# Row layout of an expert pair and the widths of its down product

## The chip, the cores and the metric

The kernel runs on one core of a Trainium2 chip. The metric is the device time of one launch in microseconds; lower is better. Every launch computes the whole model, so there is no warm part that is left out.

## The reference, cut to what matters

The model has eight residual blocks on x of 4 x 256 tokens with 256 features. The change touches only the last, a mixture of 64 experts in which each token goes to eight:

```python
def _L3_ffn_ref(hidden_states, gate_w, gate_proj_w, up_proj_w, down_proj_w):
    B, S, H, I, E, K = (2, 128, 256, 96, 64, 8)
    x = hidden_states.reshape(-1, h)                 # 1024 tokens
    router_logits = x @ gate_w
    routing_weights, selected = jax.lax.top_k(router_logits, K)
    routing_weights = jax.nn.softmax(routing_weights, axis=-1)
    ...
    gate = jax.lax.ragged_dot(hidden_sorted, gate_proj_w, group_sizes)
    up = jax.lax.ragged_dot(hidden_sorted, up_proj_w, group_sizes)
    down = jax.lax.ragged_dot(jax.nn.silu(gate) * up, down_proj_w, group_sizes)
    ...
    out = jnp.sum(out * routing_weights[..., None], axis=1)
    return out.reshape(b, s, h)
...
x = x + _L3_ffn_ref(_layernorm(x, axis=-1), ...)
```

So there are 8192 pairs of token and expert, 128 for an expert on average. Gate and up go from 256 features to 96, down goes from 96 back to 256.

## The kernel before

Everything up to the experts (the other seven blocks, and the routing of the eighth) is recorded by `Flow`, a small planner: each operation names its engine, an estimated cost, what it reads and what it writes, and the planner fixes one order for each engine. The routing stands in `tile3`, which runs once for each of the eight tiles of 128 tokens. It ends with the row numbers. `sel` marks the chosen experts, a product with a triangle of ones (L1599) gives `pos`, the place of a token among those of its expert, and `first` holds a number for each expert, made once at the start by an iota (L323). VectorE computes `ok` (L1604: chosen, and place under CAP = 192), then `v = first - pos` (L1606), times `ok` (L1607); `max` sorts the eight values of a token (L1608). The row of a choice is `slots = NROWS - v` (L1615). After that come `m` (L1622) and ACT's exponential (L1627) for the weights of the choices, and POOL's indirect DMAs (L1677), eight a tile, which scatter the normed tokens to the rows of `hs` in HBM. A last column of each row, HW = 257, holds the index of the result in `yd`; rows that no token takes hold an index out of bounds, so that nothing is written for them.

Each expert has 192 rows of `hs`, two experts are a pair, and there are 32 pairs. A count of choices that found no row (L1791 to L1797) decides whether a general path is run; it is not run here. From L1766 on PSUM and SBUF are laid out anew, and the order on PE, ACT, DVE, POOL and SP is as written. For each pair p:

- `load_rows` (L1779) brings the pair's 384 rows as [128 partitions, RPP = 3 rows]: partition q has the rows 3q, 3q+1 and 3q+2. Rows are consecutive by expert, so partitions 0 to 63 hold the first expert and 64 to 127 the second.
- `rows_turned` (L1839) turns them with six TensorE transposes to `hbT` [feature, j, q], copied out of PSUM by ACT (L1923) and DVE (L1924), one pair ahead.
- gate and up (L1912): for each of the two experts two matmuls each with 96 weight columns and 192 moving columns, which are hbT's three runs of 64. f32 throughout.
- ACT's silu gives `g` (L1918), DVE's product `act` (L1920), of shape [96, 2, 3, 64].
- the down product (L1930): for each j of 3 and each expert i, act[:, i, j, :] (96 x 64) is the stationary operand and the expert's down weights (96 x 256) move; the result goes to rows i*64 to i*64+63 of the PSUM tile `y`. j = 0 and 1 share one tile, j = 2 has another.
- the copies out of PSUM to `yb` (L1935; ACT has j = 1), and three indirect DMAs of POOL (L1937), which put the 128 rows of each j to `yd` by the indices in the loaded rows. Those indices lie in the same partitions and the same j as the results.
- SP then issues the load of the rows of pair p + 6, the weights of later experts, and at certain pairs loads of finished results from `yd`, which DVE (L1873) and PE (L1878) add to x with their weights.

On PE, the order inside the loop is: gate and up of pair p, the transposes of pair p + 1, the down product of pair p.

Of the kernel before, what the change touches and what calls it, by code (L numbers as in the profile page):

```python
# [23 lines left out]
I32 = mybir.dt.int32  # L24
AF = mybir.ActivationFunctionType
ALU = mybir.AluOpType
AX = mybir.AxisListType

P = 128
# [17 lines left out]
E3, I3, K3 = 64, 96, 8  # L47
ORDERED = {mybir.EngineType.PE, mybir.EngineType.DVE, mybir.EngineType.Activation,
           mybir.EngineType.Pool}
GROUP, WEIGHTS, FIRST = 4, 6, 2  # L50
# [5 lines left out]
ON_PE = (3, 4, 5, 6, 7)  # L56
CAP = 192
RPP = 2 * CAP // P
NROWS = E3 * CAP
NPAIR = NTOK * K3  # L60
NSTAGE = 9
# [169 lines left out]
def model(ctx: ExitStack, tc: tile.TileContext, a: dict, out: bass.AP):  # L231
    nc = tc.nc
    PSUM = bass.MemoryType.PSUM

    const = ctx.enter_context(tc.tile_pool(name="const", bufs=1))
# [11 lines left out]
    def held(pool, shape, name, dtype=F32):  # L247
        return pool.tile(shape, dtype, tag=name, name=name)
# [4 lines left out]
    def x_t(t):  # L253
# [20 lines left out]

    hs = dram.tile([NROWS, HW], F32, tag="hs", name="hs")
    yd = dram.tile([NPAIR, D], F32, tag="yd", name="yd")
# [10 lines left out]
    q1 = [q1_both[:, k, :] for k in range(2)]  # L287
    q12 = held(early, [P, 2 * RPP * HW], "q12", BF16)
    q2 = [held(early, [P, 2 * I2], f"q2{k}", BF16) for k in range(3)]
# [28 lines left out]
        channel_multiplier=-1,  # L318
    )
    onesb = held(const, [P, P], "onesb", BF16)  # L320
    nc.gpsimd.memset(onesb, 1.0)
    first_i = held(const, [P, E3], "first_i", I32)
    nc.gpsimd.iota(first_i, pattern=[[-CAP, E3]], base=NROWS, channel_multiplier=0)  # L323
    first = held(const, [P, E3], "first")
    nc.vector.tensor_copy(first, first_i)
    sel = held(const, [P, NT, E3], "sel", BF16)
    rwo = held(const, [P, NT, E3], "rwo")
# [3 lines left out]
    for j in range(K3):  # L331
        nc.gpsimd.memset(bound[:, j : j + 1], float(NROWS - BOUND[j] * CAP))
    choice_w = held(const, [P, NT, K3], "choice_w")
# [24 lines left out]
    ps = banks.tile([P, 2, NT], F32, tag="bank0", name="ps_far")  # L358
# [56 lines left out]
    def layers(nk):  # L415
# [25 lines left out]
        def bank(shape, name):  # L441
            return ("bank", shape, name)
# [31 lines left out]
        def loader():  # L474
# [18 lines left out]
            def simple(name, c):  # L493
# [1061 lines left out]
        def tile3(t, q, lane, left):  # L1555
# [9 lines left out]
            y = yield Op(PE, 3.5, (u, BO3), new=[bank([P, D], "ps_y")])  # L1565
# [9 lines left out]
            rows = hx.ap.rearrange("p (j d) -> p j d", j=K3)  # L1575
# [5 lines left out]
            hT, rest = w[:, :D].rearrange("p (c r) -> p c r", c=2), w[:, D + E3 : D + 2 * E3]  # L1581
            lg, ok, v = w[:, D : D + E3], w[:, D + 2 * E3 : D + 3 * E3], w[:, D + 3 * E3 : D + 4 * E3]
# [14 lines left out]
            ps = yield Op(PE, 0.06 * (t + 1), SEL[: t + 1], new=[bank([P, E3], "ps_pos")])  # L1597
# [4 lines left out]
            pos, places = ps.ap, Buf()  # L1602
            yield Op(DVE, 1.4, (ps, SEL[t]), (places,))
            nc.vector.scalar_tensor_tensor(ok, pos, float(CAP), sel[:, t, :], ALU.is_lt, ALU.mult)  # L1604

            nc.vector.tensor_sub(v, first, pos)  # L1606
            nc.vector.tensor_mul(v, v, ok)  # L1607
            nc.vector.max(top[:, 8 : 8 + K3], v)  # L1608

# [3 lines left out]
            nc.vector.tensor_reduce(spilt, rest[:, 1 : 1 + K3], AX.X, ALU.max)  # L1613
            nc.vector.tensor_scalar(rest[:, 0:1], spilt, float(NROWS), float(NROWS), ALU.mult, ALU.add)
            nc.vector.tensor_scalar(  # L1615
# [55 lines left out]
        def scatter(t, hx, rows, row_data, places, at):  # L1671
            for j in range(K3):
# [6 lines left out]
                    out_offset=bass.IndirectOffsetOnAxis(ap=slots[:, t, j : j + 1], axis=0),  # L1679
                    in_=rows[:, j, :], in_offset=None, bounds_check=NROWS - 1, oob_is_err=False,  # L1680
                )
# [43 lines left out]
    def ps_mm(shape, name):  # L1725
        return psum.tile(shape, F32, tag="mm", name=name, bufs=4)
# [4 lines left out]
    def ps_acc(shape, name):  # L1731
        return psum.tile(shape, F32, tag="acc", name=name, bufs=2)
# [19 lines left out]
    def moe_tile(shape, tag, bufs):  # L1752
        return moe.tile(shape, F32, tag=tag, name=tag, bufs=bufs)
# [4 lines left out]
    def load_weights(k):  # L1758
# [31 lines left out]
    ps = ps_acc([P, NT], "ps_over")  # L1790
# [6 lines left out]
    with tc.If(rv > 0):  # L1797
# [7 lines left out]
        with tc.For_i(0, E3, 1) as e:  # L1805
            dn = moe_tile([I3, D], "dn_left", 1)
            nc.sync.dma_start(dn, a["w3_dn"][:, bass.ds(e, 1), :].rearrange("p e d -> p (e d)"))
            gu = moe_tile([P, 4 * I3], "gu_left", 1)
            nc.sync.dma_start(gu, a["w3_gu"][:, bass.ds(e, 1), :, :].rearrange("p e k i -> p (e k i)"))
            for c in range(NCH):  # L1810
                pg, pu = ps_mm([I3, CH], "ps_g3"), ps_mm([I3, CH], "ps_u3")
# [6 lines left out]
                g = moe_tile([I3, CH], "g_left", 1)  # L1818
                nc.scalar.activation(g, pg, AF.Silu)
                nc.vector.tensor_mul(g, pu, g)  # L1820
                for k in range(TPC):
                    t = c * TPC + k
                    y = ps_acc([P, D], "ps_y")
# [10 lines left out]
    def rows_turned(p):  # L1834
        hb, hbT = hbs[p], moe_tile([P, 2, RPP, P], "hbT", 2)
        tps = [ps_tp([P, RPP, P], "tp_hb") for _ in range(2)]
        for dc, tp in enumerate(tps):
            for j in range(RPP):
                nc.tensor.transpose(tp[:, j, :], hb[:, j, dc * P : (dc + 1) * P], ident)  # L1839
        return hbT, tps  # L1840
# [54 lines left out]
    def experts():  # L1895
        for p in range(in_early, AHEAD):
            load_rows(p)
        load_weights(FIRST)
        load_weights(FIRST + 1)

        nc.scalar.activation(silu, mhalf, AF.Silu)
        hbT, tps = rows_turned(0)
        nc.scalar.copy(hbT[:, 0], tps[0])
        nc.vector.tensor_copy(hbT[:, 1], tps[1])
        for p in range(n_pairs):
            e = 2 * p
            gu, dn = weights[e // GROUP]
            pg, pu = ps_mm([I3, 2, RPP, P // 2], "ps_g3"), ps_mm([I3, 2, RPP, P // 2], "ps_u3")
            for k, ps in enumerate((pg, pu)):
                for i in range(2):  # L1910
                    for dc in range(2):
                        nc.tensor.matmul(  # L1912
                            ps[:, i], gu[:, (e + i) % GROUP, 2 * k + dc, :],
                            hbT[:, dc, :, i * (P // 2) : (i + 1) * (P // 2)],
                            start=dc == 0, stop=dc == 1,
                        )
            g = moe_tile([I3, 2, RPP, P // 2], "g4", 2)
            nc.scalar.activation(g, pg, AF.Silu)  # L1918
            act = moe_tile([I3, 2, RPP, P // 2], "act3", 2)
            nc.vector.tensor_mul(act, pu, g)  # L1920
            if p + 1 < n_pairs:
                hbT, tps = rows_turned(p + 1)
                nc.scalar.copy(hbT[:, 0], tps[0])  # L1923
                nc.vector.tensor_copy(hbT[:, 1], tps[1])  # L1924
            yb = moe_tile([P, RPP, D], "yb", 3)
            for js in ((0, 1), (2,)):
                y = ps_acc([P, len(js), D], "ps_y")
                for k, j in enumerate(js):
                    for i in range(2):
                        nc.tensor.matmul(  # L1930
                            y[i * (P // 2) : (i + 1) * (P // 2), k], act[:, i, j, :],
                            dn[:, (e + i) % GROUP, :], start=True, stop=True,
                        )
                for k, j in enumerate(js):
                    (nc.scalar.copy if j == 1 else nc.vector.tensor_copy)(yb[:, j, :], y[:, k, :])  # L1935
            for j in range(RPP):
                put = nc.gpsimd.indirect_dma_start(  # L1937
                    out=yd[:, :],
                    out_offset=bass.IndirectOffsetOnAxis(
                        ap=hbs[p][:, j, D : D + 1].bitcast(I32), axis=0  # L1940
                    ),
                    in_=yb[:, j, :], in_offset=None, bounds_check=NPAIR - 1, oob_is_err=False,
                )
                tc.declare_no_dep(put.ins, group="back", reason="distinct rows")
                tc.add_to_no_dep_group("back", put.ins)
                backs.append(put.ins)

            n = len(on_pe)
            for t, j in on_pe[p * n // n_pairs : (p + 1) * n // n_pairs]:
                nc.vector.tensor_scalar(  # L1950
                    diag[:, t // 2, j - ON_PE[0], :], ident, choice_w[:, t, j : j + 1], None, ALU.mult
                )
            if p + AHEAD < n_pairs:
                load_rows(p + AHEAD)
            k = FIRST + 2 + p if p < WEIGHTS - 2 else p // 2 + WEIGHTS if p % 2 else 0
            if k and k < E3 // GROUP:
                load_weights(k)
# [113 lines left out]
```

## Time and profile before

| what | value |
|---|---|
| median of 4 runs | 686.26 us |
| lowest and highest | 678.46 and 688.81 us |
| the profiled execution | 680.24 us |
| its span, first to last profiled instruction | 678.5 us |
| granted TensorE clock, mean | 0.965 |
| PE busy, weight loads busy | 609.1 us (90%), 469.5 us (69%) |
| DVE, ACT, POOL busy | 462.4, 349.5, 401.3 us |
| down product L1930 | 384 PE instructions, 395 ns each (388 with the first pairs' weights) |
| gate and up L1912 | 512 PE instructions, 326 to 339 ns each, those of the first pairs to 419 |

The time is 1.7 us above the span in the profiled execution. A matmul's recorded duration runs until its result is out; the distance from one start to the next is shorter, since matmuls overlap. A weight load (PEld) is listed beside the matmul that uses it. In a timeline the first column is the start in us, the second the length from first start to last end of a group, "x12" the number of instructions in it, and the bracket the idle time before it with what ended it. The experts' stage lies from 488 us, where the first transposes start, to 659 us, where the last put is issued; the sum of the results follows until 675 us.

### The profile page before, as it was taken

What the parts mean: (1) busy time and instruction counts of PE and PEld (TensorE: products, weight loads), DVE (VectorE), ACT (ScalarE), POOL (GpSimd) and SP (SyncE); (2) the same over time, 40 slices, a digit from 0 to 9 for tenths busy, and PEclk for the clock granted to TensorE, in tenths of its full rate; (3) what the DMA queues carried; (4) which work ended last, traced back from release to release, by engine and by line L of the source; (5) the groups of instructions that cost most, each with busy time, mean ns of one, the idle gap of its engine ahead of it and who ended that gap; (6) DMA issues with size and microseconds to landing.
All of it is one profiled execution on the core that took longest, in us unless ns stands there. A gap on an engine that the chain in (4) does not pass through costs nothing. (4 is left out here: it accounts for less than half of the span.)

```text
span 678.5 us, 11498 instructions
## 1 busy us (share of the span) xinstructions
PE 609.1 (90%) x3831; PEld 469.5 (69%) x3844; DVE 462.4 (68%) x1172; ACT 349.5 (52%) x898; POOL 401.3 (59%) x524
## 2 busy tenths in 40 slices
PE   5997699989999999999998799877399999989966
PEld 4763377766787778778787678664287877868754
DVE  5679857875968796699799788876334334333655
ACT  1143258869788854567875685665322222222210
POOL 6997985045364536647248748766645565646650
PEclk9999899989999999999998999898599999989997
DMA  8999999401100230000030201222499878766567
GB/s 288 372 385 227 226 215 238 132 25 47 63 2 1 63 109 2 0 1 1 2 102 31 87 24 39 74 77 78 140 291 334 290 253 275 247 193 219 172 207 253
DMA packets 57059, 98.15 MB, mean 145 GB/s; under 512 B 7121, under 2 KB 39624, under 8 KB 56992
## 3 DMA queue, kind: packets, MB, share of 16 engines
q1 hardware_dynamic: 47072, 78.40, 38.9%
q0 software_dynamic: 7680, 16.84, 7.2%
q10 hardware_dynamic: 2240, 2.10, 0.9%
q8 instruction: 32, 0.52, 0.3%
q14 instruction: 35, 0.29, 0.1%
HBM read 58.42 MB, written 43.07 MB: 150 GB/s over the span
## 5 line engine op out<-in xcount | busy, mean ns | idle before, releaser
L1937 POOL DMA_INDIRECT yd<-yb,hb x84 | 82.8, 986 | 62.4 <-DVE yb L1935 42.2
L1677 POOL DMA_INDIRECT hs<-hx,slots x64 | 66.6, 1040 | 26.1 <-issue 11.7
L861 POOL TENSOR_TENSOR st<-st,mhalf 128x1 f32<-128x1 f32 x56 | 32.8, 590 | 61.6 <-DVE st L857 47.8
L1920 DVE TENSOR_TENSOR act<-ps_u,g 96x384 f32<-96x384 f32 x32 | 17.7, 553 | 63.5 <-issue 32.7
L1510 ACT ACTIVATE e<-ps_s,nm 128x128 f32<-128x128 f32 x128 | 45.5, 387 | 15.7 <-DVE nm L1504 13.9
L1477 POOL TENSOR_TENSOR q<-rt 64x512 f32<-64x512 f32 x32 | 42.7, 1333 | 12.0 <-DVE rt L1473 7.4
L1930 PE MATMUL ps_y<-wt,act 96*64 96x256 f32 x336 | 43.5, 395 | 5.9 <-DVE act L1920 4.3
L1912 PE MATMUL ps_g<-hbT,wt 128*96 128x192 f32 x224 | 43.8, 339 | 0.0
L1935 DVE COPY yb<-ps_y 128x256 f32<-128x256 f32 x64 | 25.2, 422 | 26.1 <-PE ps_y L1930 24.4
L1912 PEld LDWEIGHTS ps_g<-hbT,wt 128*96 128x96 f32 x224 | 34.6, 165 | 11.3 <-issue 10.8
L1912 PE MATMUL ps_u<-hbT,wt 128*96 128x192 f32 x224 | 41.0, 326 | 0.0
L1935 ACT COPY yb<-ps_y 128x256 f32<-128x256 f32 x32 | 11.9, 372 | 53.8 <-DVE yb L1935 34.4
L1498 PEld LDWEIGHTS ps_s<-keys,q 128*128 128x128 f32 x256 | 36.0, 203 | 1.4
L1930 PEld LDWEIGHTS ps_y<-wt,act 96*64 96x64 f32 x336 | 22.0, 138 | 21.1 <-DVE act L1920 9.4
L1912 PEld LDWEIGHTS ps_u<-hbT,wt 128*96 128x96 f32 x224 | 36.4, 163 | 0.0
L1498 PE MATMUL ps_s<-keys,q 128*128 128x128 f32 x256 | 36.0, 287 | 0.0
L1422 POOL TENSOR_TENSOR hh<-g,v 128x512 f32<-128x512 f32 x16 | 20.2, 1273 | 25.4 <-ACT g L1420 16.5
L1923 ACT COPY hbT<-tp_hb 128x384 f32<-128x384 f32 x31 | 14.8, 478 | 36.0 <-PE tp_hb L1839 19.1
L1239 ACT ACTIVATE qT<-tp_q,rnd 128x512 bf16<-128x512 f32 (+2 forms) x48 | 25.7, 567 | 13.9 <-PE tp_q L1235 13.8
L1918 ACT ACTIVATE g<-ps_g 96x384 f32<-96x384 f32 x32 | 15.6, 486 | 33.6 <-PE ps_g L1912 15.2
L1463 PE MATMUL ps_q<-qc,wq 96*128 96x256 f32 x128 | 30.4, 381 | 0.0
L864 DVE TENSOR_SCALAR h<-x,st 128x256 f32<-128x256 f32 x56 | 27.0, 494 | 5.0 <-POOL st L861 4.8
(345 smaller groups left out, 1727.9 us busy)
## 6 DMA issues: line engine op xcount, KB each, us to landing
hs<-blank_row SPq DMA_DIRECT2D x1, 12336.0 KB
hb<-hs SPq DMA_DIRECT2D x28, 385.5 KB
wt<-in_w_gu SPq DMA_DIRECT2D x14, 768.0 KB
yd<-blank SPq DMA_DIRECT2D x1, 8192.0 KB
wt<-yd SPq DMA_DIRECT2D x6, 1024.0 KB
wt<-in_w_dn SPq DMA_DIRECT2D x14, 384.0 KB
wo<-in_w_o SPq DMA_DIRECT2D x2, 1024.0 KB
w<-in_w SPq DMA_DIRECT2D x2, 704.0 KB
```

The source lines that it names most:

```text
L861: nc.gpsimd.tensor_tensor(s[:, 8:9], s[:, 7:8], mhalf, ALU.pow)
L864: nc.vector.tensor_scalar(h[:, k, :], x_t(t), ss[k][:, 6:7], ss[k][:, 8:9], ALU.subtract, ALU.mult)
L1239: nc.scalar.activation(qT[:, 4 * i : 4 * i + full, :], tp.ap[:, :full, :], AF.Identity, bias=rnd[:, 1:2])
L1463: nc.tensor.matmul(ps.ap[:, k, :], w[:, hp * P : (hp + 1) * P], qc.ap, start=True, stop=True)
L1477: nc.gpsimd.tensor_add(qv(q[i])[r, hps, :], t0[r], t1[r])
L1498: nc.tensor.matmul(s.ap[:, k, :], qv(q[hd % 2])[:, hd // 2, rows], keys3[:, hd % 2, b * S : b * S + nk * P], start=False, stop=k == n - 1,)
L1510: nc.scalar.activation(wide[:, k, :], s.ap[:, k, :], AF.Exp, bias=nm[:, k : k + 1], accum_out=tot[:, k : k + 1],)
L1677: put = nc.gpsimd.indirect_dma_start(out=hs[:, :], out_offset=bass.IndirectOffsetOnAxis(ap=slots[:, t, j : j + 1], axis=0), in_=rows[:, j, ...
L1912: nc.tensor.matmul(ps[:, i], gu[:, (e + i) % GROUP, 2 * k + dc, :], hbT[:, dc, :, i * (P // 2) : (i + 1) * (P // 2)], start=dc == 0, stop= ...
L1930: nc.tensor.matmul(y[i * (P // 2) : (i + 1) * (P // 2), k], act[:, i, j, :], dn[:, (e + i) % GROUP, :], start=True, stop=True,)
L1935: (nc.scalar.copy if j == 1 else nc.vector.tensor_copy)(yb[:, j, :], y[:, k, :])
L1937: put = nc.gpsimd.indirect_dma_start(out=yd[:, :], out_offset=bass.IndirectOffsetOnAxis(ap=hbs[p][:, j, D : D + 1].bitcast(I32), axis=0), ...
```

## The change

The rows of a pair are placed differently inside its block of 384. Before, row r of a pair is its r-th row in order of expert and place. After, the r-th goes to row 3*(r mod 128) + r div 128, so that after the load [128, 3] the first expert fills j = 0 (128 rows) and the first 64 partitions of j = 1, and the second expert the other 64 partitions of j = 1 and j = 2. In `tile3` this needs a jump in the row number at place 128 of the first expert and at place 64 of the second: `first` becomes two tables (start value and place of the jump), and L1606's one subtraction three VectorE instructions. Gate and up read one run of 192 columns for each expert instead of three of 64. The down product becomes four matmuls instead of six: 128 rows of the first expert (j = 0), 64 and 64 (j = 1), 128 rows of the second (j = 2). The costs that the planner is given stay the same, and so does its order.

```diff
+STEP = RPP * P - 1
...
-    first_i = held(const, [P, E3], "first_i", I32)
-    nc.gpsimd.iota(first_i, pattern=[[-CAP, E3]], base=NROWS, channel_multiplier=0)
-    first = held(const, [P, E3], "first")
+    first_i = held(const, [P, 2, E3], "first_i", I32)
+    second = RPP * (CAP - P) + 1
+    pairs = first_i.rearrange("p k (e i) -> p k e i", i=2)
+    for i in range(2):
+        nc.gpsimd.iota(
+            pairs[:, 0, :, i], pattern=[[-2 * CAP, E3 // 2]], base=NROWS - i * second,
+            channel_multiplier=0,
+        )
+        nc.gpsimd.iota(
+            pairs[:, 1, :, i], pattern=[[0, E3 // 2]], base=CAP - P if i else P, channel_multiplier=0
+        )
+    first = held(const, [P, 2, E3], "first")
     nc.vector.tensor_copy(first, first_i)
...
-            nc.vector.tensor_sub(v, first, pos)
+            nc.vector.tensor_tensor(v, pos, first[:, 1, :], ALU.is_ge)
+            nc.vector.scalar_tensor_tensor(rest, pos, -float(RPP), first[:, 0, :], ALU.mult, ALU.add)
+            nc.vector.scalar_tensor_tensor(v, v, float(STEP), rest, ALU.mult, ALU.add)
             nc.vector.tensor_mul(v, v, ok)
...
-            pg, pu = ps_mm([I3, 2, RPP, P // 2], "ps_g3"), ps_mm([I3, 2, RPP, P // 2], "ps_u3")
+            pg, pu = ps_mm([I3, 2, CAP], "ps_g3"), ps_mm([I3, 2, CAP], "ps_u3")
+            rows = hbT.rearrange("p c j q -> p c (j q)")
...
                         nc.tensor.matmul(
-                            ps[:, i], gu[:, (e + i) % GROUP, 2 * k + dc, :],
-                            hbT[:, dc, :, i * (P // 2) : (i + 1) * (P // 2)],
-                            start=dc == 0, stop=dc == 1,
+                            ps[:, i, :], gu[:, (e + i) % GROUP, 2 * k + dc, :],
+                            rows[:, dc, i * CAP : (i + 1) * CAP], start=dc == 0, stop=dc == 1,
                         )
...
                 for k, j in enumerate(js):
-                    for i in range(2):
+                    for i, q in ((0, slice(0, P)),) if j == 0 else ((1, slice(0, P)),) if j == 2 else (
+                        (0, slice(0, CAP - P)), (1, slice(CAP - P, P))
+                    ):
+                        r = slice(j * P + q.start, j * P + q.stop)
                         nc.tensor.matmul(
-                            y[i * (P // 2) : (i + 1) * (P // 2), k], act[:, i, j, :],
-                            dn[:, (e + i) % GROUP, :], start=True, stop=True,
+                            y[q, k], act.rearrange("p i r -> p (i r)")[:, r], dn[:, (e + i) % GROUP, :],
+                            start=True, stop=True,
                         )
```

More of the change, by code (lines that the diff above doesn't have):

```diff
@@ L1912, in experts @@
                         nc.tensor.matmul(
-                            ps[:, i], gu[:, (e + i) % GROUP, 2 * k + dc, :],
-                            hbT[:, dc, :, i * (P // 2) : (i + 1) * (P // 2)],
-                            start=dc == 0, stop=dc == 1,
+                            ps[:, i, :], gu[:, (e + i) % GROUP, 2 * k + dc, :],
+                            rows[:, dc, i * CAP : (i + 1) * CAP], start=dc == 0, stop=dc == 1,
                         )
-            g = moe_tile([I3, 2, RPP, P // 2], "g4", 2)
+            g = moe_tile([I3, 2, CAP], "g4", 2)
             nc.scalar.activation(g, pg, AF.Silu)
-            act = moe_tile([I3, 2, RPP, P // 2], "act3", 2)
+            act = moe_tile([I3, 2, CAP], "act3", 2)
             nc.vector.tensor_mul(act, pu, g)
```

## The prediction

> **What bounds the kernel now.** I read the windows by stage first, to see whether the experts (494 to 659 us) are a TensorE stage at all.
>
> ```profile
> 500.00:550.00 50.00, 49.53 (x344) 40.21 (x342) 20.04 (x46) 13.36 (x30) 29.18 (x30) 1.00 0.93 302
> 550.00:600.00 50.00, 46.38 (x314) 36.81 (x310) 18.83 (x44) 12.30 (x28) 26.74 (x28) 0.97 0.74 248
> 600.00:640.00 40.00, 39.62 (x272) 32.18 (x270) 18.83 (x44) 10.32 (x23) 23.15 (x24) 0.99 0.63 201
> ```
>
> The columns are window, length, busy us of PE, PEld, DVE, ACT and POOL, then granted clock, DMA share and GB/s. PE is busy 49.5 of 50 us at clock 1.00, DVE 20 and ACT 13. So PE is the pacemaker, but busy PE is not streaming PE. The timeline of one pair shows how its 4.99 us are spent (start, length until the last end, count).
>
> ```profile
> 518.20 0.82 PE L1839 MATMUL tp_hb<-ident,hb 128*128 128x128 f32 x6
> 519.06 1.52 PE L1930 MATMUL ps_y<-wt,act 96*64 96x256 f32 x12
> 520.51 1.54 PE L1912 MATMUL ps_g<-hbT,wt 128*96 128x192 f32 x8
> 521.89 1.47 PE L1912 MATMUL ps_u<-hbT,wt 128*96 128x192 f32 x8
> 523.19 0.82 PE L1839 MATMUL tp_hb<-ident,hb 128*128 128x128 f32 x6
> ...
> 518.46 0.55 DVE L1920 TENSOR_TENSOR act<-ps_u,g 96x384 f32<-96x384 f32 x1 [2.17 <-issue]
> ```
>
> Three things are to be seen. First, each f32 matmul is two PE instructions: 6 give x12. Second, the twelve 64-column ones take 1.52 us. Less the last one's recorded 0.38 that leaves 1.14 from first to last start. Their starts, read one by one, come in couples 0.007 us apart, and couple to couple is 0.267 once and then 0.216 four times. The halves of the output (rows 0-63 and 64-127) run side by side. Third, act ends at 519.01 and the first ps_y starts 0.05 later: the product starts on DVE's result, not on PE's own readiness.
>
> What a 128-column matmul of these 256 moving elements costs is in two earlier groups; L1567 stands twice, once running on from other work and once after a wait.
>
> ```profile
> 348.17 1.89 PE L1463 MATMUL ps_q<-qc,wq 96*128 96x256 f32 x8
> 341.01 3.62 PE L1567 MATMUL ps_y<-bo,u 128*128 128x256 f32 x16
> 454.51 3.72 PE L1567 MATMUL ps_y<-bo,u 128*128 128x256 f32 x16 [0.61 <-ACT e L1510]
> ```
>
> L1463 is the very shape of the new product (96*128, 96x256): (1.89-0.38)/7 = 0.216 us each. The two L1567 rows differ by 0.10 (0.104 read start by start): the load of 128 columns of weights when nothing runs in front of it.
>
> Between the two widths PE leaves a hole. From the same timeline:
>
> ```profile
> 449.61 1.21 PE L1532 MATMUL tp_e<-ident,e 128*128 128x128 f32 x8
> 450.75 1.94 PE L1548 MATMUL ps_u<-e,kvc 128*64 128x512 f32 x8
> ```
>
> The last transpose starts at 449.61+1.21-0.27 = 450.55; the 64-column group starts 0.203 later, where two transposes lie 0.109 apart: **0.094 to go from 128 to 64 columns**. On the way back, the last ps_y of the pair above starts at 520.20 and ps_g at 520.51, 0.308 after it for a stream of 0.208: **0.10 to go back**. After either, the first weight load is bare: 0.05 for 64 columns (0.267 against 0.216), 0.08 for the 96 of ps_g (its second start comes 0.240 after its first, those of ps_u 0.162; so 1.54 against 1.47 for the same eight instructions), 0.104 for 128.
>
> **The change part by part.** *The down product, per pair.* Streamed time stays: before six couples of 64-column instructions, 6 x 0.216 = 1.30; after two 128-column matmuls (four instructions) and two couples, again 6 x 0.216 = 1.30. Fewer matmuls (four for six) save nothing, since those removed ran beside others. What differs is the holes.
> Before: bare load of 64 at the start 0.05, back to full width 0.10, bare load of ps_g 0.08; sum 0.23. The way in costs nothing: it is hidden by the wait for act (the last transpose starts at 518.74 and would leave the array free for 64 columns at 518.95, act allows 519.06). If act were not late, it would cost 0.09.
> After, the narrow middle product (j = 1) stands between two wide ones: bare load of 128 after the wait for act 0.104; into 64 columns 0.094, no longer hidden; bare load of 64, 0.05; back 0.10; bare load of 128 for j = 2, 0.104. ps_g then follows at equal width at no cost. Sum 0.45.
> Difference 0.22 us a pair, on the path: PE's order ps_y, ps_g, ps_u, then act, then ps_y is a ring, and the transposes lie inside its act wait. 32 x 0.22 = **7.1 us**. The holes inside a run of j = 0, 1, 2 in this order are not in the trace, so I bound them: if the inner switches and the loads after them cost nothing, what remains after is the first 0.10, and the pair is 0.13 shorter, -4.0 us; if each inner switch waits for the earlier matmul's recorded end (0.38) and the 0.055 that lies from act's end to its user, it is 0.435 from start to start where I have 0.31, 0.25 more a pair, +15.2 us in all. I take 0.22, since both switches have direct rows.
>
> The Trainium skill, "TensorEngine Tiling (Array Packing)", Key Properties, states that a change of tiling mode, not of tile, drains TensorE; it speaks against this change, which puts the narrow product between wide ones, and the rows just read agree in kind. It gives no price; by it alone the count of switches would stay at two a pair and the sum at zero, and only the trace shows that one of the two had been hidden. "TensorE: Matmul & The Clock Gate", LDWEIGHTS, gives columns/1.2 ns, 107 for 128 columns by my estimate where the rows show 104, and the sum by it would be some 0.3 us higher.
>
> *Gate and up (L1912), silu, act.* 192 moving columns in one run in place of 3 x 64 strided; instructions, shapes and counts are equal. ps_u shows 0.162 each with the strided reading, which is 192/256 of the 0.216, so no penalty that could go: 0. *Copies and puts.* yb copies, 96 indirect puts on POOL, loads and SP's queue keep number, order and size; both output banks are complete about 0.2 later after act, which is in the ring already. Live rows move (j = 0 now mostly full, j = 1 and 2 half); a put's packet of four live rows took 0.16 to 0.45 us, of blank ones 0.01, two for each DMA engine. At worst 0.3 later for j = 0, under POOL's wait for the next yb: 0.
>
> *Row numbers (L1606, eight tiles).* One DVE subtraction becomes three instructions.
>
> ```profile
> 477.06 0.23 DVE L1604 SCALAR_TENSOR_TENSOR w<-ps_pos,sel 128x64 f32<-128x64 f32 x1 [0.58 <-PE ps_pos L1599]
> 477.21 0.21 DVE L1606 TENSOR_TENSOR w<-first,ps_pos 128x64 f32<-128x64 f32 x1
> 477.45 0.22 DVE L1607 TENSOR_TENSOR w<-w 128x64 f32<-128x64 f32 x1
> ...
> 478.70 0.21 DVE L1622 TENSOR_SCALAR m<-top,st 128x1 f32<-128x1 f32 x1
> ...
> 479.44 0.23 DVE L1631 TENSOR_TENSOR w<-w,sel 128x64 f32<-128x64 f32 x1 [0.53 <-ACT w L1627]
> ```
>
> An independent successor starts 0.15 after the one before, a dependent one 0.24. So two more cost 0.15 + 0.24 = 0.39. Behind them stand slots (the scatter's addresses), m, ACT's exponential and then the overflow count and its branch. For the last tile that is bare, as DVE had waited 0.58 for PE just before: 0.4. For the other seven it is 2.7 at most (DVE is 81% busy from 347 to 477 us; it idles 24.8 of 130 us) and 0 at least; I keep half, 1.4, because DVE's idle times there end on engines that it feeds itself. *Start.* Three more iotas, about 0.15 each, lie under POOL's 1.50 us wait before L630 (0.45 without it); the copy of `first` doubles, 0.03. Nothing.
>
> Sum 7.1 + 0.4 + 1.4 = **8.9 us**. Against the profiled execution (680.24 us, 678.5 of it span) that is 689.1. The median of the four runs is 6.0 above it, at 686.26, and the new kernel is likely to be timed as those were: **695.2 us**, +1.3%.
>
> **The rivals.** *Dear switches (slower than 2%).* Place: before and after j = 1. Price: full wait for the earlier results, 15.2 + 1.8 = 17.0, **703.3 us**. It decides from (13.7-1.8)/32 = 0.37 us a pair. For it: nothing shows a 96-row product switched twice within 1.3 us, and both wide loads take weights from act, which was just written. Against: three places in the trace all show 0.09 to 0.10.
> *Free switches (not slower).* Loads are fetched under the couple in front, the way to ps_g is now smooth: -4.0 + 1.8, **684.1 us**. For it: wide loads in a run are wholly hidden (L1463 keeps 0.216). Against: the bare load after each switch in the pair above.
> *PE is not the ring.* The stage follows DVE or DMA and the 0.22 fits into idle time: +1.8, **688.1 us**. For it: PE idles about 0.1 before act, and some ps_y start 0.4 to 3 us late behind ACT's late silu (559.42, 597.09) or the added results (649.36). Against: other starts of ps_y stand 4.99 apart, to 0.01, and act itself hangs on ps_u.
>
> **How the numbers follow.** Forecast 0.62, dear switches 0.17, free switches 0.10, not the ring 0.11. Two per cent, 13.7 us, is about what a measurement of this kernel can tell from no change (four runs span 678.5 to 688.8). Slower by over 2% means above 700.0: 0.15 of the dear case and 0.07 of the forecast's upper end, 0.22. Faster by over 2% would need 0.43 a pair, more than all holes of before (0.23) together; 0.03 for what I don't see. Within: 0.75. The range runs from the free case, 684, to the dear case, 703.
>
> **What would show it.** In the changed profile: ps_y rows of two forms, 128-column ones 0.216 apart; ps_y to ps_y starts 5.21 us apart instead of 4.99; ps_g no longer 0.08 longer than ps_u; from the last wide j = 0 start to the narrow couple 0.31; three 128x64 DVE rows where one stood, and the first expert's transposes some 0.4 to 3 us later. Steps of 4.99 would prove the ring wrong, 4.86 the holes, 5.4 or more the price of a switch.

## The result, and the profile after

Measured against one another in the same places, the changed kernel has a median of 685.93 us (52 runs, 683.18 to 691.66) and the kernel before one of 685.6 us (78 runs, 677.7 to 694.24). The ratio is 1.0024, with a 95% interval of 1.0011 to 1.0037: **+1.6 us, where +8.9 was forecast**. The profiled execution took 684.45 us (span 682.7, granted clock 0.975), against 680.24 (678.5, 0.965) for that of before.

The windows by stage are those shown of before, now of the changed kernel (window, length, busy us of PE, PEld, DVE, ACT and POOL, clock, DMA share, GB/s).

```profile
500.00:550.00 50.00, 49.52 (x288) 38.99 (x287) 20.73 (x46) 12.90 (x29) 27.63 (x29) 1.00 0.98 316
550.00:600.00 50.00, 49.25 (x289) 39.34 (x287) 19.03 (x43) 12.61 (x29) 28.16 (x30) 1.00 0.74 245
600.00:640.00 40.00, 39.63 (x230) 31.28 (x229) 18.56 (x44) 10.15 (x23) 22.08 (x23) 1.00 0.63 210
```

The middle window is the one that differs: PE is busy 49.25 us at clock 1.00, where before it was 46.38 at 0.97. There the kernel before keeps PE idle for 3.6 us, the changed one for 0.75.

The timeline of one pair of the changed kernel (start, length until the last end, count) shows the new ring; POOL's and DVE's lines are used further down.

```profile
520.79 0.97 POOL L1956 DMA_INDIRECT yd<-yb,hb  x1 [0.30 <-issue]
520.81 0.55 DVE L1935 TENSOR_TENSOR act<-ps_u,g 96x384 f32<-96x384 f32 x1 [2.04 <-issue]
...
521.42 1.91 PE L1949 MATMUL ps_y<-wt,act 96*128 96x256 f32 x8
...
522.75 0.42 DVE L1954 COPY yb<-ps_y 128x256 f32<-128x256 f32 x1 [0.78 <-PE ps_y L1949]
...
523.17 1.47 PE L1928 MATMUL ps_g<-hbT,wt 128*96 128x192 f32 x8
...
524.47 1.46 PE L1928 MATMUL ps_u<-hbT,wt 128*96 128x192 f32 x8
...
525.77 0.82 PE L1854 MATMUL tp_hb<-ident,hb 128*128 128x128 f32 x6
...
526.63 1.70 PE L1949 MATMUL ps_y<-wt,act 96*128 96x256 f32 x7
```

ps_y to ps_y is 526.63 - 521.42 = 5.21 us, as forecast (the last line is cut by the window's end). ps_g lasts 1.47, no longer 0.08 more than ps_u. From ps_y to ps_g it is 523.17 - 521.42 = 1.75, where before it was 1.45; 0.08 of this 0.30 comes back in ps_g, and 0.22 stays. Start by start, the block reads 0.320, 0.309, 0.007, 0.260, 0.007, 0.309, 0.320 and 0.216 to ps_g: a bare load of 128 (0.216 + 0.104), the way into 64 columns (0.31), the couple, a bare load of 64 (0.05), the way back (0.31), a bare load of 128, and no hole at the end.

The row numbers of the last tile:

```profile
478.41 0.23 DVE L1618 SCALAR_TENSOR_TENSOR w<-ps_pos,sel 128x64 f32<-128x64 f32 x1 [0.28 <-PE ps_pos L1613]
478.55 0.22 DVE L1620 TENSOR_TENSOR w<-ps_pos,first 128x64 f32<-128x64 f32 x1
478.68 0.22 DVE L1621 SCALAR_TENSOR_TENSOR w<-ps_pos,first 128x64 f32<-128x64 f32 x1
478.93 0.22 DVE L1622 SCALAR_TENSOR_TENSOR w<-w 128x64 f32<-128x64 f32 x1
479.19 0.23 DVE L1623 TENSOR_TENSOR w<-w 128x64 f32<-128x64 f32 x1
```

From the first row-number operation to the product with `ok` it is 479.19 - 478.55 = 0.64, before 477.45 - 477.21 = 0.24: +0.40, the forecast term.

So every duration is there, and the sum is not. The stage as a whole tells where it went: the first and the last ps_y, of before and then of after, from the timelines.

```profile
494.10 1.52 PE L1930 MATMUL ps_y<-q,act 96*64 96x256 f32 x12
...
654.36 1.52 PE L1930 MATMUL ps_y<-wt,act 96*64 96x256 f32 x12 [0.72 <-DVE act L1920]
```

```profile
495.44 1.81 PE L1949 MATMUL ps_y<-q,act 96*128 96x256 f32 x8
...
658.85 1.91 PE L1949 MATMUL ps_y<-wt,act 96*128 96x256 f32 x8 [0.71 <-DVE act L1935]
```

After: 163.41 us for 31 steps; 31 x 5.216 is 161.7, so 1.7 beside the ring. Before: 160.26; 31 x 4.989 is 154.7, so **5.6 us beside the ring**, mostly in four steps (pairs 13, 20, 21 and 30, counted from 0: 0.45, 2.75, 1.64 and 0.74 over). The late pair 30 is in every run below, where `act` stands behind DVE's additions; the other three, 4.84 us, are this execution's own. Between the two profiled executions the stage grew by 3.15 us instead of 7, and its first ps_y starts 1.34 later, as the row numbers' 1.8 would have it. The question is what the 5.6 us of before are, and why a longer ring has less of it.

### The profile page after: what moved, and what is told of

The parts are those of the page before. It is cut to its first block, busy times and chain, and to the rows that moved or that the text cites. A ratio compares the mean times of both kernels' runs of the same rounds, so it can differ in the third digit from the quotient of the medians.

```text
span 682.7 us, 11261 instructions
## 1 busy us (share of the span) xinstructions
PE 614.0 (90%) x3703; PEld 469.1 (69%) x3716; DVE 467.4 (68%) x1188; ACT 349.7 (51%) x898; POOL 401.5 (59%) x527
## 5 line engine op out<-in xcount | busy, mean ns | idle before, releaser
L1949 PE MATMUL ps_y<-wt,act 96*128 96x256 f32 (+1 forms) x224 | 53.5, 418 | 3.3 <-DVE act L1935 2.0
L1524 ACT ACTIVATE e<-ps_s,nm 128x128 f32<-128x128 f32 x128 | 45.6, 392 | 16.1 <-DVE nm L1518 13.8
L1954 DVE COPY yb<-ps_y 128x256 f32<-128x256 f32 x64 | 27.1, 425 | 30.7 <-PE ps_y L1949 29.9
L1949 PEld LDWEIGHTS ps_y<-wt,act 96*128 96x128 f32 (+1 forms) x224 | 22.2, 161 | 30.0 <-issue 23.5
L1928 PE MATMUL ps_g<-hbT,wt 128*96 128x192 f32 x224 | 41.3, 326 | 0.3 <-DVE hbT L1939 0.3
L1928 PEld LDWEIGHTS ps_g<-hbT,wt 128*96 128x96 f32 x224 | 36.3, 163 | 2.9 <-DVE hbT L1939 0.6
L1436 POOL TENSOR_TENSOR hh<-g,v 128x512 f32<-128x512 f32 x16 | 20.2, 1274 | 25.3 <-ACT g L1434 16.5
L1253 ACT ACTIVATE qT<-tp_q,rnd 128x512 bf16<-128x512 f32 (+2 forms) x48 | 25.7, 567 | 13.8 <-PE tp_q L1249 13.7
L1581 PE MATMUL ps_y<-bo,u 128*128 128x256 f32 x128 | 29.5, 382 | 1.4 <-ACT u L1566 1.3
```

Source lines behind the costliest of these rows:

```text
L1253: nc.scalar.activation(qT[:, 4 * i : 4 * i + full, :], tp.ap[:, :full, :], AF.Identity, bias=rnd[:, 1:2])
L1524: nc.scalar.activation(wide[:, k, :], s.ap[:, k, :], AF.Exp, bias=nm[:, k : k + 1], accum_out=tot[:, k : k + 1],)
L1581: nc.tensor.matmul(y.ap, u[:, hp, :], bo3[:, hp, :], start=hp == 0, stop=hp == H3 // 2 - 1)
L1928: nc.tensor.matmul(ps[:, i, :], gu[:, (e + i) % GROUP, 2 * k + dc, :], rows[:, dc, i * CAP : (i + 1) * CAP], start=dc == 0, stop=dc == 1,)
L1949: nc.tensor.matmul(y[q, k], act.rearrange("p i r -> p (i r)")[:, r], dn[:, (e + i) % GROUP, :], start=True, stop=True,)
```

## The experiments

Five jobs ran, each on another chip, and in each the kernels stand beside runs of the kernel before on that chip. The kernel before does not take the same time everywhere, and this is what the answer hangs on. The stage column is the last ps_y minus the first in that run's profile.

| chip, median of before | kernel | layout, ring | difference, 95% interval (us) | stage (us) |
|---|---|---|---|---|
| 13, 680.0 | e4, before again | old, 4.99 | 0.1 (-1.9, 2.2) | 156.1 |
| 13 | e3, before, longer ring | old, 5.21 | 5.0 (2.3, 7.8) | 163.1 |
| 13 | e2, six narrow matmuls | new, 4.99 | -1.4 (-3.3, 0.5) | 156.4 |
| 13 | e1, narrow product first | new, 5.02 | 0.3 (-1.8, 2.4) | 159.8 |
| 3, 670.7 | f1, after | new, 5.21 | **9.0 (7.5, 10.5)** | 162.7 |
| 3 | f2, before again | old, 4.99 | -0.2 (-1.0, 0.6) | 155.4 |
| 3 | f3, before, longer ring | old, 5.21 | 5.8 (4.8, 7.0) | 162.2 |
| 3 | f4, before, shorter ring | old, 4.56 | -10.8 (-12.4, -9.3) | 147.1 |
| 2, 670.8 | g1, after | new, 5.21 | **8.5 (7.0, 10.1)** | 163.0 |
| 2 | g2, before again | old, 4.99 | -0.4 (-1.3, 0.5) | 155.4 |
| 2 | g3, before, longer ring | old, 5.21 | 5.6 (3.9, 7.2) | 162.2 |
| 2 | g4, six narrow matmuls | new, 4.99 | 1.3 (0.1, 2.5) | 155.4 |
| 1, 685.3 | h1, after | new, 5.21 | **2.2 (0.0, 4.4)** | 163.1 |
| 1 | h2, before, longer ring | old, 5.21 | 4.5 (1.9, 7.0) | 163.2 |
| 1 | h3, six narrow matmuls | new, 4.99 | -0.8 (-3.2, 1.6) | 160.6 |
| 4, 681.0 | i1, before, two puts | old, 4.99 | -3.7 (-5.9, -1.6) | 155.4 |
| 4 | i2, after, two puts | new, 5.21 | 4.2 (2.2, 6.3) | 162.9 |
| 4 | i3, before, shorter ring | old, 4.56 | -2.7 (-5.2, -0.3) | 156.1 |

### The holes, taken out or put in alone (chip 13)

e1 computes j = 1 first, so that only one bare load of 128 and one switch stay inside:

```diff
-                for k, j in enumerate(js):
+                for k, j in reversed(list(enumerate(js))):
```

> The changed kernel with j = 1 (64 and 64) ahead of the wide j = 0 and j = 2: the way into 64 columns lies under the wait for act again, and only 0.03 us a pair is left of the added holes, so ps_y starts should stand 5.01 us apart (5.21 in the changed kernel, 4.99 before). Theory A, slack: before, something other than PE's ring already held the experts' stage at about 5.17 us a pair on average, so PE's 0.22 mostly replaced waiting. Then this kernel is no faster than the changed one by more than 2 us: 684 to 687. Theory B, offset: the new layout saved about 5 us elsewhere and the holes cost their full 7. Then taking the holes away gives 6 us: about 680.

e2 keeps the new rows and goes back to six matmuls of 64 columns:

```diff
-                    for i, q in ((0, slice(0, P)),) if j == 0 else ((1, slice(0, P)),) if j == 2 else (
-                        (0, slice(0, CAP - P)), (1, slice(CAP - P, P))
-                    ):
+                    for i, q in zip(((0, 0), (0, 1), (1, 1))[j], (slice(0, CAP - P), slice(CAP - P, P))):
```

> The changed kernel's layout and row numbers with the down product as six 64-column matmuls again (two for the one expert in j = 0 and in j = 2): PE's block is that of before, 4.99 us a pair. Theory A: 684 to 687, with late completions of ps_y and stalls as before. Theory B: about 679, since layout's gain stays and the holes are gone.

e3 is the kernel before with one couple of half the moving columns more, which computes part of j = 2 a second time:

```diff
+                    for i in range(2 if j == 2 else 0):
+                        nc.tensor.matmul(
+                            y[i * (P // 2) : (i + 1) * (P // 2), k, : D // 2], act[:, i, j, :],
+                            dn[:, (e + i) % GROUP, : D // 2], start=True, stop=True,
+                        )
```

> The kernel before with one more pair of 64-column matmuls over 128 of the 256 output columns after j = 2 (written twice, same values): 0.216 us more PE work a pair, old layout, no change of width. The ring is 5.20 us, as in the changed kernel. Theory A: the time stays within 2 us of before (685 to 687). Theory B: without the layout's gain it costs 32 x 0.216 = 6.9 us, 692 to 693.

e4 is the kernel before, unchanged:

> The kernel before, unchanged, for a second profile: ratio 1.000. Theory A: the pairs again average 5.1 to 5.25 us though most steps of PE's ring are 4.99, because of late completions and a few long stalls, and these stalls need not be at the same pairs. Theory B: the average is near 5.0 and the stalls of the first profile (5.6 us in all) were a rare accident.

In the profiles the ring is 5.017 us for e1, 4.99 for e2 and 5.208 for e3, so the order of the products is indeed all there is to the 0.22. But e3 cost +5.0 us, most of its 32 x 0.216 = 6.9, on a chip where the kernel before stands 5.6 us lower than in the first comparison and its stage runs nearly clean (156.1). As written, all three came out nearer to theory B: e3 because theory A had expected little there, e1 and e2 because their medians, 679.8 and 678.0, are those that B had named. But every one of these times was counted from a kernel before at 686, and here it stands at 680, so they decide nothing. e1's profile has 4.3 us beside its ring (pairs 20, 30 and 31), which is left open. What was missing is the changed kernel itself on the same chip.

### The changed kernel where the kernel before is quick (chips 3 and 2)

f4 leaves the couples of j = 2 out, a third of the down product; the copy of j = 2 reads the rows of j = 0:

```diff
             for js in ((0, 1), (2,)):
+                if j0 := js[0]:
+                    nc.vector.tensor_copy(yb[:, j0, :], y[:, 0, :])
+                    break
                 y = ps_acc([P, len(js), D], "ps_y")
```

> The changed kernel, unchanged, beside the lengthened and the shortened kernel before. Theory A (the cost depends on how far the kernel before stalls on its own in that job: where it runs its ring of 4.99 cleanly and measures about 680 us, the 0.22 a pair is paid nearly whole; where it measures about 686 us it is already waiting for something outside TensorE and the 0.22 replaces that waiting): +5 to +7 us if the kernel before has a median near 680 here, +0 to +3 if it is near 686; either way within 1.5 us of the lengthened kernel f3. Theory B (the new row layout saves about 5 us elsewhere and the holes cost their full 7): +1.6 us wherever it runs, about 5 us below f3.

> The kernel before, unchanged, for a profile of the same chip and the noise between two equal kernels. Both theories: ratio 1.000 +- 0.003. Theory A: if the median is near 680, steps of 4.99 us with under 2 us of excess over 32 pairs; if near 686, 5 us of excess or more.

> The kernel before with one more couple of 64-column matmuls over half the moving columns a pair (a second time, same result), which lengthens the ring by 0.216 us without any change of layout. Theory A: +5 to +7 us where the kernel before is near 680, +0 to +3 where it is near 686, within 1.5 us of f1. Theory B: +6.9 wherever it runs, 5 us above f1.

> The kernel before without the couples of j = 2 (two of six); the copy of j = 2 reads the rows of j = 0 instead, so that the copies and the puts stay. This leaves out a third of the down product. The ring is 2 x 0.216 = 0.43 us shorter, 4.56 us a pair. Theory A: if TensorE's ring is all that binds, -13.8 us; where the kernel before is near 686 something beside TensorE (the loop of copies and three puts, about 5.04 us a pair in the first profile) holds it, and the gain stays under 5 us. Theory B: -13.8 us wherever it runs.

f1 is +9.0 us where the kernel before takes 670.7: the forecast's 8.9, on a chip where the kernel before has nothing beside its ring (155.4 for 31 steps; 154.7 plus the 0.68 of pair 30). f3 is 3.2 below f1, and not 5 above it, so theory B is out: the new layout saves nothing there. Theory A's "within 1.5 us of f1" is missed too; in the stage f1 and f3 differ by 0.5 only (162.7, 162.2), and f1's first ps_y starts 2.1 later. With f4 the time follows the ring down as well, -10.8 for 0.43 a pair. Of the 13.8 that this would be in all, the rest is lost to other waits: f4's stage has 5.8 us beside its ring, 2.9 of it at pairs 8 and 9, where PE waits for loads of rows.

Chip 2 is another one on which the kernel before is quick. The job there repeats three of the kernels and adds e2's:

> Once more the changed kernel, in a two by two table of layout (old, new) and length of the ring (4.99, 5.21 us a pair). Theory A (ring): +6 to +9.5 us if the kernel before stands at 670 to 680 us here; if it stands near 686, +0 to +3 and within 1.5 us of g3. Theory B' (the new layout removes stalls that only some jobs have): if the kernel before stands near 686, +0 to +3, but 4 us or more below g3.

> The kernel before unchanged, for its profile in the same place. Both: ratio 1.000 +- 0.003.

> Old layout, ring lengthened by 0.216 us a pair. Both theories: +6 to +7 us where the kernel before stands at 670 to 680 us. Where it stands near 686: theory A +0 to +3 (the longer ring replaces waiting), theory B' +5 to +7.

> New layout, but the down product in six 64-column matmuls as before, so that the ring is 4.99 us. Where the kernel before stands at 670 to 680 us: -2 to +2 (theory A: +1.8 of row numbers; theory B' somewhat less). Where it stands near 686: theory A 0 to +2, theory B' -4 to -7.

It splits the forecast into its terms: the layout and its row numbers alone (g4) cost 1.3 us, where 1.8 was forecast, and the wide products on top of it 8.5 - 1.3 = 7.2, where 7.1 was. The intervals of the two leave the 7.2 some 2 us to either side; the stages, one profile each, differ by 7.6.

### The two by two table where the kernel before is slow (chip 1)

> The changed kernel beside two that share one half of it each: h2 its ring (5.21 us a pair, old layout), h3 its layout (new rows, ring 4.99). Where the kernel before stands at 670 us: +8.5 again, all theories. Where it stands at 680 to 686 us: theory A (the longer ring replaces waiting) +0 to +3; theory B' (the new layout removes stalls of these chips) +0 to +4, as the ring's 7 less 4 to 7.

> Where the kernel before stands at 670 us: +6, all theories. Where it stands at 680 to 686 us: theory A +0 to +3, equal to h1 within 1.5; theory B' +5 to +7, 4 or more above h1.

> Where the kernel before stands at 670 us: +1.3, all theories. Where it stands at 680 to 686 us: theory A 0 to +2; theory B' -3 to -7.

At 685.3 us for the kernel before the first comparison comes back: +2.2. h2's +4.5 lies outside theory A's 0 to 3 and 2.3 above h1, which fits neither theory well; but their stages take the same 163.2 and 163.1, and h2's profile begins its experts 5.6 us later than h1's (502.64 against 497.00), although h1 has the longer row numbers ahead of them. In the stage, then, by one profile each, the longer ring alone takes away what is special to this chip, as theory A has it; what h2 loses ahead of the experts is not explained. Whether the layout adds 1 or 2 us of gain on such chips (g4 +1.3, h3 -0.8, e2 -1.4) is within the intervals and stays open. h3 shows what is special: with a ring of 4.99 its stage takes 160.6, like the first profile of before. From h3 to h1 the stage thus grows by 2.5 us, where on chips 3 and 2 it grows by 7.3 and 7.6 from before to after.

### What comes late on those chips

Most starts of the products are 4.99 apart there too. What is late is the news of their end. The timeline of before, two pairs of it:

```profile
529.04 1.52 PE L1930 MATMUL ps_y<-wt,act 96*64 96x256 f32 x12
...
530.42 0.76 DVE L1935 COPY yb<-ps_y 128x256 f32<-128x256 f32 x2 [0.83 <-PE ps_y L1930]
...
531.12 0.97 POOL L1937 DMA_INDIRECT yd<-yb,hb  x1 [1.49 <-DVE yb L1935]
...
532.40 0.97 POOL L1937 DMA_INDIRECT yd<-yb,hb  x1 [0.31 <-issue]
...
533.68 0.97 POOL L1937 DMA_INDIRECT yd<-yb,hb  x1 [0.30 <-issue]
...
534.03 1.52 PE L1930 MATMUL ps_y<-wt,act 96*64 96x256 f32 x12
...
535.52 0.76 DVE L1935 COPY yb<-ps_y 128x256 f32<-128x256 f32 x2 [0.94 <-PE ps_y L1930]
```

The first copy of yb (j = 0) starts 535.52 - 534.03 = 1.49 us after the product's start, a pair earlier 1.38, and in f2 1.13 every time. DVE had been idle for 0.94 us, waiting for ps_y alone. It starts 0.87 after the end of the last put (533.68 + 0.97 = 534.65). In h3 the same lines stand like this:

```profile
527.17 0.76 DVE L1952 COPY yb<-ps_y 128x256 f32<-128x256 f32 x2 [0.92 <-PE ps_y L1947]
...
527.87 0.97 POOL L1954 DMA_INDIRECT yd<-yb,hb  x1 [1.50 <-DVE yb L1952]
...
529.15 0.97 POOL L1954 DMA_INDIRECT yd<-yb,hb  x1 [0.30 <-issue]
...
530.43 0.97 POOL L1954 DMA_INDIRECT yd<-yb,hb  x1 [0.31 <-issue]
...
532.20 0.76 DVE L1952 COPY yb<-ps_y 128x256 f32<-128x256 f32 x2 [0.95 <-PE ps_y L1947]
```

This is a loop: copy to first put 0.70, two steps of 1.28, the third put 0.97, and from its end 0.80 to the next copy: 5.03, with TensorE's 4.99 inside it. Each pair the copy comes some 0.05 later against TensorE, up to 0.58 in before and 0.68 in h3, and then falls back. In the semaphore records of the profile of before, 34 completions of PE in the stage come over 0.06 us after the end of the last row that could have sent them, and 20 of these 34 come 0.76 to 0.85 us after the end of the latest put. (The trace has only 130 records for the 186 completions of the stage; in every profile but those of chips 2 and 3 some are missing.) In the profiles of after and of h1, with a ring of 5.21, the first copy is late in one pair and in three, and on time (1.23 to 1.33 after the product's start) in all others; it then stands 522.75 - (520.79 + 0.97) = 0.99 after the put, outside the loop. In f2 and f4 all completions are recorded (186 and 154) and none is late, and in f4, whose ring is shorter still, the copy follows the put's end (555.21 + 0.97) by 0.32:

```profile
555.21 0.97 POOL L1940 DMA_INDIRECT yd<-yb,hb  x1 [0.31 <-issue]
...
555.37 1.08 PE L1933 MATMUL ps_y<-wt,act 96*64 96x256 f32 x8
...
556.50 0.42 DVE L1938 COPY yb<-ps_y 128x256 f32<-128x256 f32 x1 [0.58 <-PE ps_y L1933]
```

So on chip 3 a put holds nothing up. Where it does, the 0.05 a pair is not all of the loss. Where puts follow one another from pair to pair, with 0.3 us between them, other completions are caught, and the chain to the next product breaks. Such a row stands about pair 18, and there the first copy is late, by 0.15 to 1.85 us, in every profile but those of chips 2 and 3 and the two with two puts a pair. The changed kernel has it too, its one late pair. DVE's copy of hbT waits 1.99 us after the transposes' end, to 1.10 after the last put's, the copies of yb stand behind it, and the next step is 0.57 longer:

```profile
588.35 0.82 PE L1854 MATMUL tp_hb<-ident,hb 128*128 128x128 f32 x6
...
589.09 0.97 POOL L1956 DMA_INDIRECT yd<-yb,hb  x1 [0.30 <-issue]
...
591.16 0.56 DVE L1939 COPY hbT<-tp_hb 128x384 f32<-128x384 f32 x1 [2.01 <-PE ps_y L1949]
```

The costliest case is pair 20 of before, the largest of its four excesses:

```profile
590.26 0.97 POOL L1937 DMA_INDIRECT yd<-yb,hb  x1 [0.30 <-DVE hbT L1924]
...
590.80 1.54 PE L1912 MATMUL ps_g<-hbT,wt 128*96 128x192 f32 x8
...
591.54 0.97 POOL L1937 DMA_INDIRECT yd<-yb,hb  x1 [0.31 <-issue]
...
592.82 0.97 POOL L1937 DMA_INDIRECT yd<-yb,hb  x1 [0.30 <-issue]
...
594.10 0.97 POOL L1937 DMA_INDIRECT yd<-yb,hb  x1 [0.30 <-issue]
595.02 0.49 ACT L1918 ACTIVATE g<-ps_g 96x384 f32<-96x384 f32 x1 [3.71 <-PE tp_hb L1839]
596.49 0.55 DVE L1920 TENSOR_TENSOR act<-ps_u,g 96x384 f32<-96x384 f32 x1 [4.95 <-issue]
...
597.09 1.27 PE L1930 MATMUL ps_y<-wt,act 96*64 96x256 f32 x6 [2.80 <-DVE act L1920]
```

ps_g ends at 590.80 + 1.54 = 592.34 and POOL puts with gaps of 0.31 at most until 595.07; silu starts at 595.02, 2.68 us after its input was done. act and the next ps_y wait for it. And this waiting is paid twice, since the clock is granted at half for 3.4 us afterwards, which makes up the 1.64 of pair 21 (the window's row, clock third from its end); in h3, e1 and i3 a late step of 1.7 us or more is likewise followed by 3.4 us at half:

```profile
597.50:600.80 3.30, 3.30 (x16) 1.88 (x13) 1.30 (x4) 0.37 (x1) 0.97 (x1) 0.50 0.63 215
```

### Taking the puts away (chip 4)

That the puts are the cause is so far only read from their times. i1 and i2 leave out the put of j = 2 in the kernel before and in the changed one, so a third of the results is not stored; i3 is f4's kernel.

```diff
-            for j in range(RPP):
+            for j in range(2):
                 put = nc.gpsimd.indirect_dma_start(
...
+            backs.append(put.ins)
```

> The kernel before with the puts of j = 0 and 1 alone; the results of j = 2 are not stored, so POOL has 64 puts instead of 96. Theory P (where the kernel before takes 680 us or more, the loop of copies and three puts, 5.04 us a pair, holds the pairs, and stalls come out of it): -4 to -8 there, and no growing lateness of the first ps_y; -1 to -2 where the kernel before takes 670 us (one put less at the end). Rival (the puts only happen to end in step, and something else makes these chips slow): -1 to -2 everywhere.

> The changed kernel with the same two puts. Theory P: about 7 to 8.5 us above i1 on any chip, since without the third put nothing but TensorE's ring is left to hold the pairs. Rival: 2 to 4 us above i1 where the kernel before takes 680 us or more, 8.5 where it takes 670.

> The kernel before without the couples of j = 2 once more (a third of the down product left out, ring 4.56 us, three puts): -11.5 where the kernel before takes 670 us, as measured. Where it takes 680 us or more: theory P 0 to -4, as the loop of the puts stays at 5.04; rival -9 to -12.

i1's time by itself decides nothing: 3.7 us lies between theory P's 4 to 8 and the rival's 1 to 2, its interval reaches into both, and part of it is the end of the kernel, which from the last ps_y on takes 22.74 us in i1 and 24.15 to 25.35 in the profiles of the kernel before. No profile of the kernel before was taken on chip 4, so how late its copies were there is not known; on chip 13, where it takes 680.0, its stage was nearly clean. What i1's profile shows is that with two puts the stage is clean (155.4, each step 4.99 but that to pair 30) and the first copy comes 1.13 us after its product in all 32 pairs, 2.04 after the end of the last put (528.85 + 0.97):

```profile
528.85 0.97 POOL L1937 DMA_INDIRECT yd<-yb,hb  x1 [0.30 <-DMA wt<-in_w_dn]
...
530.73 1.51 PE L1930 MATMUL ps_y<-wt,act 96*64 96x256 f32 x12
531.86 0.86 DVE L1935 COPY yb<-ps_y 128x256 f32<-128x256 f32 x2 [0.58 <-PE ps_y L1930]
```

The changed kernel with two puts stands 4.2 + 3.7 = 8.0 us above i1 (by the ratios, 1.0062 - 0.9945; the interval is some 3 us to either side), and its stage 7.5 above i1's: **with two puts a pair the cost forecast is paid whole, on a chip where the kernel before takes 681 us**. This is as theory P has it, and not the rival's 2 to 4. That less is paid on this same chip with three puts was not measured. i3 speaks for theory P more clearly. The same kernel with the same ring of 4.56 goes through the stage in 147.1 us on chip 3, here in 156.1; the first and last ps_y of f4 and of i3:

```profile
488.63 1.08 PE L1933 MATMUL ps_y<-q,act 96*64 96x256 f32 x8
...
635.69 1.08 PE L1933 MATMUL ps_y<-wt,act 96*64 96x256 f32 x8 [0.86 <-DVE act L1920]
```

```profile
493.96 1.08 PE L1933 MATMUL ps_y<-q,act 96*64 96x256 f32 x8
...
650.08 1.08 PE L1933 MATMUL ps_y<-wt,act 96*64 96x256 f32 x8 [0.86 <-DVE act L1920]
```

156.1 / 31 = 5.04 us a pair for a ring of 4.56, on average the length of the loop. It is an average only: thirteen steps of i3 take 4.56 us, the others up to 7.2, and the first copy comes from 1.13 to 2.98 us after its product, where in f4 it is 1.13 each time. So late completions hold this kernel on chip 4, but not by a steady loop. A ring that is shorter by 0.43 is worth 2.7 us there in all, and 10.8 on chip 3.

No version that does the whole work is shown to be faster than the kernel before; six narrow matmuls on the new rows (e2, g4, h3) come nearest, from -1.4 to +1.3.

## Why the prediction was right or wrong

*The terms.* The ring's 5.21, the holes one by one (0.104, 0.31, 0.05, 0.31, 0.104), the ps_g that is no longer longer, the 0.40 of the last tile's row numbers: all as forecast. In us, 7.1 for the holes was 7.2 (g1 less g4), 1.8 for the row numbers 1.3 (g4), and the sum of 8.9 was 9.0 and 8.5 on chips 3 and 2. Neither the dear nor the free switches came. The hole of 0.09 to 0.10 at a change of width stands at both switches around j = 1 too (0.309 from start to start, for a stream of 0.216). The Trainium skill, "TensorEngine Tiling (Array Packing)", Key Properties, states that a change of tiling mode drains TensorE, and these rows agree.

*The step that failed* is the one that put the 0.22 "on the path" of the kernel before, 32 times, and set it on top of a median of 686.26; where the forecast was made, 3.15 us of 7.1 were paid in the stage. It was argued from starts: the rival that TensorE is not the ring was set aside because "other starts of ps_y stand 4.99 apart, to 0.01". They do, and it proves little. TensorE waits for act and not for yb, so a loop behind it that needs 5.03 lets it run at 4.99 for some pairs, and late completions then take time back in a stall. That the prediction priced copies and puts at nothing, "under POOL's wait for the next yb", belongs to the same step: that wait, 1.49 us in the rows above, is a part of the loop. Two readings of the profile shown would have told: the stage took 160.26 us where its steps add to 154.7, and the copy of yb started 1.38, then 1.49 after its product. I had seen the late starts at 559.42 and 597.09 and counted them for the rival, but priced the forecast as if the changed kernel would keep them. It does not: 5.21 is longer than the loop, and 5.6 us beside the ring became 1.7. That the puts make these completions late is likely from their times, from i1 and from i3, but the same kernel was not profiled with and without the third put on one chip.

*The median.* That "the new kernel is likely to be timed as those were" carried 6.0 us from profile to median over to the changed kernel. Against the larger comparison the kernel before stands 5.4 above its profile and the changed one only 1.5. That before's share is the same waiting is likely, since its single runs spread over 16.5 us and the changed kernel's over 8.5, but it is not shown: no profile of one of its longer runs was read.

*The rival* that was closest, "PE is not the ring", had the price, +1.8 for the row numbers alone against the +1.6 measured, and in part the place, the late ps_y. That the prices agree is partly luck, since its mechanism, idle time in which the 0.22 fits, is not what happened: the steps are 5.21, not 4.99, and what made room for them lay in three stalls of the kernel before (pairs 13, 20 and 21).

*What stays open*: why TensorE's completions come late behind puts in the first profile, on chip 1 (h3) and on chip 4 (i3, no profile of before there), little on 13, and not on 2 and 3; whether it is POOL's instruction or the transfers that it starts, since i1 and i2 leave out both; which operations are caught and which are not (in the same profile of before many completions fall within 0.65 us after a put and are not late); and how much of the difference of 15 us between chips in the kernel before lies ahead of the experts, where the first ps_y starts at 487.6 to 491.3 on the two quick chips and at 494 or later on the others. On chip 13 the stage of before is only 0.7 us longer than on chips 2 and 3, so there hardly any of the 9 us between them lies in it.

## What to carry to other kernels

Equal steps between starts show that an engine runs at its pace, not that it sets the pace: add the steps over the stage, compare with the stage's length, and look whether the first user of its results drifts against it. A cost on the faster of two loops that differ by 1% (4.99 and 5.03 here) may be paid only in part, so price it against the longer loop too. And where a kernel's time differs by 2% from chip to chip, a change has to be tried on more than one: the same edit was +1.6 and +9.0 us.

## What the runs showed of the hardware

- On some chips a completion of TensorE becomes visible late, often only 0.76 to 0.85 us after the end of POOL's latest indirect put (20 of 34 late ones in the profile of before), or when a row of puts ends (ps_g's of 592.34, 2.68 us late); on two others none is late, with 0.32 us between a put and the copy. In the two profiles with two puts a pair none was late. The cause is not known.
- The kernel before took 670.7, 670.8, 680.0, 681.0 and 685.3 us on five chips. Its single runs lay within 3.1 us of these on the first two and within 6 on the others.
- The switch between 128 and 64 stationary columns costs 0.09 to 0.10 us each way, and the load after it is bare: 0.05 for 64 columns, 0.104 for 128. A wide product in place of two narrow ones that run side by side saves no time (0.216 either way) and brings these holes.
